# Second expert layer: value projections a quarter later, and pools that wait tile by tile for the stage before

## The chip, the cores and the metric

The program runs on one core of a Trainium2 chip. The core has five engines, each of which works off its own list of instructions in order: PE (TensorE, matrix products into PSUM), DVE (VectorE), ACT (ScalarE), POOL (GpSimd) and SP (SyncE, which here only issues DMA transfers). The metric is the device time of one execution in microseconds (us), the median of three runs. Everything is float32.

## The reference

The input `x` has 4 batches of 512 tokens with 256 channels. Four layers are added to it in turn: a cross attention, a mixture of experts, a second cross attention with a long convolution and a feed-forward net, and an attention whose value and output projections are chosen among eight experts. The change is in this last layer:

```python
# x: layer-normed input (4, 512, 256); H = 16 heads, DH = 64, E = 8 experts, K = 2
q = einsum('btc,hdc->bhtd', x, Wq);  k = einsum('btc,hdc->bhtd', x, Wk)
w, sel = top_k(einsum('btc,hec->bthe', x, Ws), K)            # two experts per token and head
mix_v  = einsum('bthk,bthke->bthe', sigmoid(w), one_hot(sel, E))
proj_v = einsum('btc,edc->bted', x, Wv)                      # a value per token and expert
v      = einsum('bthe,bted->bhtd', mix_v, proj_v)            # mixed for each head
probs  = softmax(einsum('bhid,bhjd->bhij', q * DH**-0.5, k))
attn   = einsum('bhij,bhjd->bihd', probs, v)
_, sel_o = top_k(einsum('btc,hec->bthe', x, Wd), K)
mask_o = one_hot(sel_o, E).sum(axis=3)
out    = einsum('bthe,bthd,efd->bthf', mask_o, attn, Wo).sum(axis=2)
```

## The kernel before

The four layers are four stages, one after the other. Each stage opens its own pools of SBUF and PSUM memory and closes them at its end, so a stage's pools lie where those of the stages before lay. The tokens `xr` (16 tiles of 128 tokens) stay in SBUF throughout.

**The stage before, "the old stage" below** (lines 1820 to 2009), is the second cross attention's convolution and feed-forward. Its SBUF pools are `y_w` (weights, in the order `fwd` 16 KB for each partition, `wfi` and `wfo` 4 KB each, a few bytes of `gate`, six rows of 1 KB among which `row_go` and `row_bo`, `inv` 16 KB, and more), `y_1` and `y_2`. Ahead of them lies the pool `keep`, with 4 KB of `kT4` and 16 KB of `ctT`, 20.5 KB in all. Its PSUM pools are `y_a` (six banks) and `y_t` (two). For each batch it ends with the products `po` (L2001), their addition (L2002), a layer norm into `yo` (ACT, L1908 and L1909), two operations of POOL that scale and shift `yo` with `row_go` and `row_bo` (L2005, L2006) and four POOL additions into `xr` (L2008).

**The last stage** (lines 2014 to 2252) opens `d_w` (weights), `d_1`, `d_2` (two buffers for each tag), `d_3` (four buffers of the tag `tmp`) in SBUF, and `d_m` (four single banks: `mm`, `pp`, `acc`, `ao`), `d_s` and `d_t` (two each) in PSUM. A pool is opened by default so that whoever first touches one of its tiles waits until all the work on every older pool under it is done. The four weights `d_wv`, `d_wq`, `d_wk` and `d_wo` (4, 8, 8 and 4 KB) are loaded on SP's queue at L2027. The order of PE, DVE and ACT is the order of the program text (`manual_schedule`); POOL and SP are ordered by the planner.

A *pair* `u` is two heads of one batch, eight pairs for each batch, 32 in all. A pair is worked off in four *quarters* `c`. In each quarter the loop at L2216 writes, in this order:

1. `scores(u + 1, c)`: two products `pss` on PE, for each a row maximum `dnm` on DVE (L2119) and an exponential `pe` on ACT (L2121). The bank ring of `pss` has two slots.
2. In quarters 1 and 2, `by_expert(u - 1)`: in quarter 1 a transpose `ao` on PE, two small DVE operations `drs` and `dmw`, and in each of the two quarters two DVE products `tmp2` (L2169, tag `tmp`) with a POOL addition each into `agg` (L2170).
3. A share of the *fill*, the preparation of the next batch (below).
4. In quarters 0 and 2, half of `pair_in(u + 2)`: the query or key product (`pq`, `pk`, L2070 and L2076) in the bank `mm` and its copy by ACT.
5. Output products of the batch before, now and then.
6. `transposed(u, c)` and `gather`: PE transposes with copies by ACT, and the product with the values.

The fill for the next batch is `batch_in(b + 1)`: layer norm, gates, choice of the experts, and then four times `mixed(b, qt)`, one for each 128 tokens. `mixed` makes the value projection `pp` (L2047, one bank, one buffer), and mixes it for all heads: a DVE product for each of eight experts e, the first (L2057) straight into the value tile `dv`, the other seven (L2060) into a `tmp` buffer, from which POOL adds it into `dv` (L2061). `tmp` and `tmp2` share one ring of four buffers, so DVE can be four such products ahead of POOL, no more.

Each step of the fill yields its cost in the author's own units. In each quarter `upto` (L2185) takes steps while its credit is above zero; a quarter's credit is 7.2, 1.3, 1.3 and 7.2 for c = 0 to 3, and what is overdrawn is carried on. Written out, this places the value projection of the first tile (`qt` = 0) of the next batch in quarter 0 of pair 3, and those of the other three in quarter 0 of pairs 4, 5 and 6, each directly behind the last product (e = 7) of the tile before it, which reads the same bank. The last three products of the fourth tile are in quarter 0 of pair 7.

For the very first batch there is no earlier stage to hide the fill in: `mixed(0, 0)` is interleaved with the first scores (L2203 to L2207) and the other three are run whole in the quarters of pair 0 (L2225).

Of the kernel before, what the change touches and what calls it, by code (L numbers as in the profile page):

```python
# [752 lines left out]
def kernel(ctx: ExitStack, tc: tile.TileContext, a: dict, out: bass.AP):  # L753
# [115 lines left out]
    with ExitStack() as st:  # L869
        p1 = st.enter_context(tc.tile_pool(name="f_1", bufs=1))  # L870
# [949 lines left out]
    with ExitStack() as st:  # L1820
        wp = st.enter_context(tc.tile_pool(name="y_w", bufs=1))
        p1 = st.enter_context(tc.tile_pool(name="y_1", bufs=1))
        p2 = st.enter_context(tc.tile_pool(name="y_2", bufs=2))
# [188 lines left out]


    with ExitStack() as st:
        wp = st.enter_context(tc.tile_pool(name="d_w", bufs=1))
        p1 = st.enter_context(tc.tile_pool(name="d_1", bufs=1))
        p2 = st.enter_context(tc.tile_pool(name="d_2", bufs=2))
        p3 = st.enter_context(tc.tile_pool(name="d_3", bufs=4))
        ps_m = st.enter_context(tc.tile_pool(name="d_m", bufs=1, space=PSUM))
        ps_s = st.enter_context(tc.tile_pool(name="d_s", bufs=2, space=PSUM))  # L2020
        ps_t = st.enter_context(tc.tile_pool(name="d_t", bufs=2, space=PSUM))
# [20 lines left out]

        def mixed(b, qt):

            pp = ps_m.tile([P, SE, SD], F32, name="pp", tag="pp")
            for k in range(2):
                nc.tensor.matmul(  # L2047
                    pp.rearrange("p e d -> p (e d)"), xnTs[b][:, k, qt * P : (qt + 1) * P], wv[:, k, :],
                    start=(k == 0), stop=(k == 1),
                )  # L2050
            yield 0.8
            v_t = p2.tile([P, SH, SD], F32, name=f"dv{qt}", tag=f"dv{qt}")
            for e in range(SE):
                m_w = mixes[b][:, qt * SH : (qt + 1) * SH, e].unsqueeze(2).to_broadcast([P, SH, SD])
                p_w = pp[:, e, :].unsqueeze(1).to_broadcast([P, SH, SD])
                if e == 0:
                    tt(v_t, p_w, m_w, ALU.mult)  # L2057
                else:
                    tmp = p3.tile([P, SH, SD], F32, name="tmp", tag="tmp")
                    tt(tmp, p_w, m_w, ALU.mult)  # L2060
                    nc.gpsimd.tensor_tensor(v_t, v_t, tmp, ALU.add)  # L2061
                yield 2.2
            vs[b, qt] = v_t
# [44 lines left out]
        def scores(u, it):  # L2108
            qT, kT = qks[u]
            if it == 0:  # L2110
                sums[u] = small.tile([P, QT, 2], F32, name="dsums", tag="dsums")
                nms[u] = small.tile([P, QT, 2], F32, name="dnm", tag="dnm")
            pss = [ps_s.tile([P, S], F32, name="pss", tag="pss") for _ in range(2)]
            for j in range(2):
                rows = slice(64 * j, 64 * j + SD)
                nc.tensor.matmul(pss[j], qT[rows, it * P : (it + 1) * P], kT[rows, :], start=True, stop=True)  # L2116
            for j in range(2):
                nm = nms[u][:, it, j : j + 1]
                nc.vector.tensor_reduce(nm, pss[j], AX.X, ALU.max, negate=True)  # L2119
                pe = p2.tile([P, S], F32, name="pe", tag=f"pe{it}{j}")  # L2120
                nc.scalar.activation(pe, pss[j], AF.Exp, bias=nm, accum_out=sums[u][:, it, j : j + 1])  # L2121
                pes[u, it, j] = pe
# [62 lines left out]
        def upto(g, us):  # L2185

            while us > 0:
                n = next(g, None)
                if n is None:
                    return 0.0  # L2190
                us -= n
            return us

        def batch_in(b):
            yield from inputs(b)
            yield from gates_in(b)
            yield from gates(b)
            for qt in range(QT):
                yield from mixed(b, qt)

        run(pair_in(0))
        scores(0, 0)
        fill = mixed(0, 0)  # L2203
        for c in range(1, QT):
            upto(fill, 4.0)
            scores(0, c)
        run(fill)  # L2207
        run(pair_in(1))
        values0 = [mixed(0, qt) for qt in range(1, QT)]
        outs = iter(())  # L2210
        ins = {}
        fill, credit = iter(()), 0.0
        experts = iter(())
        for u in range(NP + 1):
            b, m = divmod(u, NH)
            for c in range(QT):  # L2216
# [9 lines left out]
                if (m, c) == (1, 0) and b + 1 < B:  # L2226
                    fill, credit = batch_in(b + 1), 0.0
                if m:

                    credit = upto(fill, credit + (1.7, 0.3, 0.3, 1.7)[c] * FILL / STEPS)  # L2230
# [126 lines left out]
```

## Time and profile before

| | us |
|---|---|
| median of 3 runs (lowest, highest) | 3442.59 (3435.63, 3444.97) |
| profiled execution, its own time | 3443.15 |
| its span, first to last instruction | 3441.0 |
| PE busy (share of the span) | 2920.9 (85%) |
| DVE busy | 2301.1 (67%) |
| ACT busy | 1606.6 (47%) |
| POOL busy | 1001.1 (29%) |
| mean granted TensorE clock | 0.910 |

The old stage ends and the last stage begins at about 2540 us of the span, so the last stage is some 900 us of it. The shares above are means over four quite different stages. In the lines of the profile L is a line of the kernel, `out<-in` are tiles, and `[idle before <-releaser]` is how long the engine had stood idle and what ended that. A line of the timeline may merge several like instructions (x2, x7); its two first numbers are then the start of the first and the time to the end of the last.

### The profile page before, as it was taken

The page shows a single profiled execution, that of the slowest core. Times are in us where ns is not written, and L with a number is a line of the kernel's source. Part 1 is how long each engine was busy: PE and PEld are TensorE (multiplying, and loading weights), DVE is VectorE, ACT ScalarE, POOL GpSimd, SP SyncE. Part 2 cuts the span into 40 slices and gives each one's busy share as a digit, 9 for nine tenths or more (in the row PEclk, how much of TensorE's full clock was granted, in tenths as well). Part 3 has the DMA queues.
Part 4 walks back from the last instruction along what each step waited for, and adds up shares of the span by engine and source line. Part 5 has one row for each costly group of instructions (what it writes and reads, how often), then busy time and mean ns, then how long its engine had stood idle before and what let it go on. Part 6 is the DMA issues. An engine that isn't in the chain of part 4 may idle for free. (4 is left out here: it accounts for less than half of the span.)

```text
span 3441.0 us, 42208 instructions
## 1 busy us (share of the span) xinstructions
PE 2920.9 (85%) x15886; PEld 1637.5 (48%) x15886; DVE 2301.1 (67%) x3887; ACT 1606.6 (47%) x3307; POOL 1001.1 (29%) x747
## 2 busy tenths in 40 slices
PE   7999999999968996787978776789766888788798
PEld 3333333333347983565555555566533334344354
DVE  7666666666468984989989896343445765657654
ACT  2555555555625773555555553122323454454454
POOL 2011001100016763100000000133335781845835
PEclk9999999999958998988889998899887898898899
DMA  3001000000017882000000002100000000000000
GB/s 83 25 14 28 4 11 14 14 8 7 2 56 240 286 280 69 26 15 1 1 15 1 1 1 56 50 0 1 0 37 0 1 1 7 1 4 4 1 7 7
DMA packets 59156, 118.25 MB, mean 34 GB/s; under 512 B 16594, under 2 KB 32732, under 8 KB 58940
## 3 DMA queue, kind: packets, MB, share of 16 engines
q0 software_dynamic: 24736, 74.46, 6.9%
q1 hardware_dynamic: 33564, 40.43, 3.9%
q8 instruction: 129, 2.11, 0.3%
q14 instruction: 87, 0.71, 0.1%
q10 hardware_dynamic: 640, 0.54, 0.1%
HBM read 97.16 MB, written 9.31 MB: 31 GB/s over the span
## 5 line engine op out<-in xcount | busy, mean ns | idle before, releaser
L265 DVE TENSOR_REDUCE mx<-pss 128x1 f32<-128x512 f32 x768 | 492.6, 684 | 261.7 <-PE pss L261 257.8
L311 ACT ACTIVATE pT<-pst 128x512 f32<-128x512 f32 (+1 forms) x832 | 449.8, 596 | 405.3 <-PE pss L261 299.4
L308 PE MATMUL pst<-qm,kT 32*128 32x512 f32 (+1 forms) x1664 | 507.3, 635 | 1.4 <-ACT pT L311 0.7
L261 PE MATMUL pss<-kT,qT 32*128 32x512 f32 x1536 | 494.0, 642 | 4.1 <-DMA kT<-kc 3.5
L1113 PE MATMUL sum<-dg,e 128*128 128x128 f32 (+1 forms) x1664 | 265.3, 322 | 129.2 <-ACT dg L1089 128.9
L2170 POOL TENSOR_TENSOR agg<-agg,tmp 128x1024 f32<-128x1024 f32 x112 | 263.2, 2381 | 278.8 <-DVE tmp L2169 278.7
L1113 PEld LDWEIGHTS sum<-dg,e 128*128 128x128 f32 (+1 forms) x1664 | 237.3, 225 | 186.3 <-ACT dg L1089 154.3
L2121 ACT ACTIVATE pe<-pss,dnm 128x512 f32<-128x512 f32 x256 | 173.5, 683 | 270.5 <-DVE dnm L2119 270.3
L2119 DVE TENSOR_REDUCE dnm<-pss 128x1 f32<-128x512 f32 x256 | 164.5, 683 | 176.8 <-PE pss L2116 176.4
L2061 POOL TENSOR_TENSOR dv<-dv,tmp 128x1024 f32<-128x1024 f32 x112 | 262.9, 2349 | 62.0 <-DVE tmp L2060 38.5
L308 PEld LDWEIGHTS pst<-qm,kT 32*128 32x128 f32 (+1 forms) x1664 | 150.7, 180 | 267.5 <-ACT pT L311 242.8
L318 PE MATMUL acc<-pT,v 128*32 128x512 f32 (+1 forms) x1664 | 221.7, 605 | 0.3 <-ACT ou L325 0.3
L2116 PE MATMUL pss<-dkT,dqT 64*128 64x512 f32 x512 | 169.0, 659 | 25.2 <-ACT pe L2121 23.8
L169 POOL DMA_DIRECT2D qT<-qc x28 | 13.7, 496 | 578.4 <-DVE qc L232 578.1
L261 PEld LDWEIGHTS pss<-kT,qT 32*128 32x128 f32 x1536 | 149.2, 185 | 33.5 <-issue 22.9
L800 POOL TENSOR_TENSOR ln_rs<-ln_ve,nhalf 128x4 f32<-128x4 f32 x32 | 34.0, 1062 | 435.2 <-DVE ln_neg L1905 371.8
L2130 ACT COPY dpT<-tp 128x512 f32<-128x512 f32 x256 | 138.1, 595 | 46.5 <-PE tp L2128 46.5
L1591 PE MATMUL pa<-xgT,wb 128*128 128x128 f32 x1248 | 155.4, 279 | 2.4 <-ACT xgT L1584 2.4
L1559 POOL DMA_INDIRECT wb<-in_f_w,w_at x117 | 137.9, 1179 | 65.4 <-issue 19.8
L2060 DVE TENSOR_TENSOR tmp<-pp,mix 128x1024 f32<-128x1024 f32 x112 | 134.1, 1218 | 30.7 <-POOL dv L2061 23.1
L1022 PE MATMUL pss<-xkT,xqT 64*128 64x512 f32 (+1 forms) x512 | 148.4, 600 | 4.9 <-ACT sc L1029 3.1
L1591 PEld LDWEIGHTS pa<-xgT,wb 128*128 128x128 f32 x1248 | 149.4, 195 | 6.0 <-ACT xgT L1584 3.1
(419 smaller groups left out, 5591.4 us busy)
## 6 DMA issues: line engine op xcount, KB each, us to landing
c<-in_ctxT SPq DMA_DIRECT2D x8, 800.5 KB
ys<-yo SPq DMA_DIRECT2D x39, 128.0 KB
c<-in_ctxT SPq DMA_DIRECT2D x8, 400.2 KB
kT<-kc SPq DMA_DIRECT2D x96, 32.0 KB
kT<-kc POOLq DMA_DIRECT2D x84, 32.0 KB, 2.2
xr<-in_x SPq DMA_DIRECT2D x16, 128.0 KB
xs<-xn SPq DMA_DIRECT2D x4, 512.0 KB
fwd<-in_dft SPq DMA_DIRECT2D x1, 2048.0 KB
```

The lines of the kernel that those rows point to most:

```text
L261: nc.tensor.matmul(pss[:, :wd], qT[rows[j], qt * P : (qt + 1) * P], kT[rows[j], o : o + wd], start=True, stop=True,)
L265: nc.vector.tensor_reduce(mx[:, gi, qt, j, n : n + 1], pss[:, :wd], AX.X, ALU.max)
L308: nc.tensor.matmul(pst[:wd, :], kTs[gi % 4][rows, c * P : c * P + wd], qms[gi][rows, :], start=True, stop=True)
L311: nc.scalar.activation(pT[:wd, j, :], pst[:wd, :], AF.Exp)
L318: nc.tensor.matmul(acc[32 * j : 32 * j + 32, :], vs[b][:wd, c, AG * g + j, :], pT[:wd, j, :], start=(c == 0), stop=(c == NG - 1), tile_pos ...
L1113: nc.tensor.matmul(pm[:w, c - 4 * n, :], e[:, c * P : c * P + w], dg, start=(h == 0 and c == 4 * n), stop=(h == 3 and c == cols[-1]),)
L1591: nc.tensor.matmul(pa[:, c, :], wbs[i, half][:, o : o + P], xTs[i][:, k, :], start=(k == 0), stop=(k == 1))
L2061: nc.gpsimd.tensor_tensor(v_t, v_t, tmp, ALU.add)
L2116: nc.tensor.matmul(pss[j], qT[rows, it * P : (it + 1) * P], kT[rows, :], start=True, stop=True)
L2119: nc.vector.tensor_reduce(nm, pss[j], AX.X, ALU.max, negate=True)
L2121: nc.scalar.activation(pe, pss[j], AF.Exp, bias=nm, accum_out=sums[u][:, it, j : j + 1])
L2170: nc.gpsimd.tensor_tensor(aggs[b][it], aggs[b][it], tmp2, ALU.add)
```

## The change

1. The four SBUF pools of the last stage are opened with `reuse_waits="tile"`: a tile that is first touched waits for the work on those old tiles that lay under it, and no longer for all work on the old pools. The three PSUM pools stay as they were.
2. `mixed` yields a step of cost 0.0 before its projection `pp`.
3. `upto` stops a quarter's share of the fill when it meets that 0.0; the credit that is left goes to the next quarter. The places where fills are run whole (`run`) pass over it.
4. The first fill of the stage, `mixed(0, 0)`, is advanced past its 0.0 once, so it starts as before.

With the credits written out again, the four projections of batches 1, 2 and 3 move from quarter 0 to quarter 1 of pairs 3, 4, 5 and 6. With each go the products that followed it in that quarter (three, two, one and one), to quarter 1 too, behind that quarter's scores, `ao` and its first two `tmp2`. From quarter 2 on every step stands where it stood, and the fill ends in quarter 0 of pair 7 in both.

```diff
-        wp = st.enter_context(tc.tile_pool(name="d_w", bufs=1))
-        p1 = st.enter_context(tc.tile_pool(name="d_1", bufs=1))
-        p2 = st.enter_context(tc.tile_pool(name="d_2", bufs=2))
-        p3 = st.enter_context(tc.tile_pool(name="d_3", bufs=4))
+        wp = st.enter_context(tc.tile_pool(name="d_w", bufs=1, reuse_waits="tile"))
+        p1 = st.enter_context(tc.tile_pool(name="d_1", bufs=1, reuse_waits="tile"))
+        p2 = st.enter_context(tc.tile_pool(name="d_2", bufs=2, reuse_waits="tile"))
+        p3 = st.enter_context(tc.tile_pool(name="d_3", bufs=4, reuse_waits="tile"))
...
         def mixed(b, qt):
 
+            yield 0.0
             pp = ps_m.tile([P, SE, SD], F32, name="pp", tag="pp")
...
                 n = next(g, None)
                 if n is None:
                     return 0.0
+                if n == 0.0:
+                    break
                 us -= n
             return us
...
         fill = mixed(0, 0)
+        next(fill)
         for c in range(1, QT):
             upto(fill, 4.0)
             scores(0, c)
```

## The prediction

> **What bounds the kernel now.** I read the page first, then the boundary between the two stages in the timeline, then who waits for whom inside the last stage, and last POOL's own timeline, since those waits pointed to it.
>
> The page's busy times come first (engine, busy us, share, instructions).
>
> ```profile
> PE 2920.9 (85%) x15886; PEld 1637.5 (48%) x15886; DVE 2301.1 (67%) x3887; ACT 1606.6 (47%) x3307; POOL 1001.1 (29%) x747
> ```
>
> PE's 85% is a mean over stages and says little about either place that the change touches. The first is the boundary; these are lines of the timeline around 2540 us.
>
> ```profile
> 2525.21 0.42 DVE L2002 TENSOR_TENSOR xt<-po,xt 128x256 f32<-128x256 f32 x1 [3.03 <-PE po L2001]
> ...
> 2531.92 0.51 ACT L1909 ACTIVATE yo<-yo,ln_rs 128x256 f32<-128x256 f32 x1
> ...
> 2534.98 2.34 POOL L2006 TENSOR_TENSOR yo<-yo,row_bo 128x1024 f32<-128x1024 f32 x1
> 2537.34 0.38 SPq L2027 DMA_DIRECT2D d_wv<-in_d_wv  x1
> 2537.39 2.77 POOL L2008 TENSOR_TENSOR xr<-xr,yo 128x256 f32<-128x256 f32 x4
> 2537.77 0.46 SPq L2027 DMA_DIRECT2D d_wq<-in_d_wq  x1
> ...
> 2544.10 3.39 PE L2070 MATMUL pq<-dxT,d_wq 128*128 128x512 f32 x4 [18.99 <-DMA d_wq<-in_d_wq]
> 2547.65 0.60 ACT L2072 ACTIVATE dqT<-pq 128x512 f32<-128x512 f32 x1 [15.22 <-PE pq L2070]
> 2548.30 1.98 PE L2076 MATMUL pk<-dxT,d_wk 128*128 128x512 f32 x4 [0.81 <-ACT dqT L2072]
> ...
> 2552.13 1.29 DVE L2119 TENSOR_REDUCE dnm<-pss 128x1 f32<-128x512 f32 x2 [24.09 <-PE pss L2116]
> ```
>
> PE stands still for 18.99 us until a weight arrives, and that transfer is issued as soon as POOL is through with L2006, the last reader of the old pools under `d_w`. DVE waits 24.09, ACT 15.22: nothing else runs here, so the boundary is on the path of the whole program.
>
> The second place is the fill. In the waits of the last stage's three fills, the projection stands out (us in total, times, longest):
>
> ```profile
> PE pp L2047 <- DVE tmp L2060: 59.2, 9, 8.7
> ```
>
> PE stands nine times before `pp`, because DVE still reads its bank. What that costs is seen on POOL, in the fill of the last batch:
>
> ```profile
> 3145.78 4.78 POOL L2061 TENSOR_TENSOR dv<-dv,tmp 128x1024 f32<-128x1024 f32 x2 [11.95 <-DVE tmp L2060]
> 3150.53 9.28 POOL L2170 TENSOR_TENSOR agg<-agg,tmp 128x1024 f32<-128x1024 f32 x4
> 3159.78 14.36 POOL L2061 TENSOR_TENSOR dv<-dv,tmp 128x1024 f32<-128x1024 f32 x6
> 3175.66 9.29 POOL L2170 TENSOR_TENSOR agg<-agg,tmp 128x1024 f32<-128x1024 f32 x4 [1.52 <-DVE tmp L2169]
> ...
> 3202.99 4.67 POOL L2170 TENSOR_TENSOR agg<-agg,tmp 128x1024 f32<-128x1024 f32 x2 [3.61 <-DVE tmp L2169]
> ...
> 3233.16 9.31 POOL L2170 TENSOR_TENSOR agg<-agg,tmp 128x1024 f32<-128x1024 f32 x4 [4.16 <-DVE tmp L2169]
> ...
> 3259.32 9.30 POOL L2170 TENSOR_TENSOR agg<-agg,tmp 128x1024 f32<-128x1024 f32 x4
> ```
>
> From 3145.78 to 3268.62 POOL rests only three times, 9.29 us in 122.84. It takes some 2.35 us for an addition, DVE 1.2 for the product behind it, and DVE stalls on the ring of four. In the fills POOL is the bound, and the PE waits matter only by POOL's gaps.
>
> **The change, part by part.** The sum is made against the profiled execution, 3443.15 us (span 3441.0, 2.15 around it), 0.56 above the median.
>
> *Weights, tile by tile.* By the sizes in the code, `d_w` (24 KB) lies on `keep` (20.5 KB) and the first 3.5 KB of `fwd`. The last reads of those are PE's: `kT4` by L1875 (last matmul at 2156.4), `ctT` by L1897 (2407.0), `fwd` by L1949 (2457.1). So the four issues (0.38 to 0.47 us each on SP) come between 2157 and 2458 and land by 2465 at the 5.9 us that `d_wq` took. SP's own rows have nothing between the last old load (2156.3) and 2537, so nothing queues behind their waits; the engines' DMA share in 2200 to 2400 is 0.00. Cost nothing; the cover is 60 us of old-stage products.
>
> *The first chain.* What is late next? PSUM still waits for its whole old pool: DVE's read at 2525.21 + 0.42 = 2525.63. There `pq` starts, warm, as PE stopped at 2525.1: 1.98 like the `pk` row, to 2527.6. Its copy `dqT` stands on ACT behind the last L1909, which ends at 2531.92 + 0.51 = 2532.43; with 0.60 it ends at 2533.03, and `pk`, which needs the same bank, starts at 2533.1. PE has then been idle 5.4 us. The row nearest to that is `pq` after 18.99 us (3.39 against 1.98), so I take 3.39: end 2536.5; `dkT` (0.58) 2537.1; `pss` (1.13) 2538.3; `dnm` starts at 2538.4 instead of 2552.13. Gain 13.7; with a warm `pk` 15.1, the upper bound. If the first chain were held until POOL's last old instruction ends (2537.39 + 2.77 = 2540.16), `dqT` would come at 2540.2 and not 2547.65: 7.4. If no wait goes, 0.
>
> The Trainium skill, "TensorE: Matmul & The Clock Gate" (section "Part 1: The HAM clock gate"), lets the clock fall to half after an idle window of about 3.4 us; by it `pk` is cold and the sum is the same 13.7, and the trace agrees, with a `pss` group that takes 2.74 and not 1.13 after 2.57 idle.
>
> *The other tiles of the first pairs.* `dqT` and `dkT` lie on `fwd` and `wfi`, free by 2458. The first `dv` lies on `row_go` and `row_bo`, so DVE's L2057 waits for L2006 (2537.32); it is due at 2554.24 − 13.7 = 2540.5. POOL's first `dv` addition is due at 2556.81 − 13.7 = 2543.1, and POOL is free at 2540.16. Slack 2.9: nothing. More semaphore waits may be written: the rows have 51 ns for one; 40 first touches on three engines would be 2 us if all were on the path, they are not, so 0.
>
> *Pair 0.* `run` passes the 0.0 and `mixed(0, 0)` is advanced by hand, so the two PE waits there (75.6 us in the whole stage less 59.2) stay.
>
> *The fills.* Twelve projections move by a quarter: on PE from ahead of `pq` to behind the next scores and `ao`; on DVE three, two, one and one products move behind two `dnm`, `drs`, `dmw` and two `tmp2`; their POOL additions (two, one, none, none; e = 0 has none) move behind two `agg` additions. No DMA moves. Nine projections had waited; what queued behind them was `pq`, transposes, the next scores, and with these DVE's next `tmp2` and so POOL.
>
> Now take quarter 0 of pair 4 in the last fill. The product e = 7 ends on DVE at 3162.18 + 1.21 = 3163.4, with POOL busy until 3174.1. Before, `pp` (3.78, cold), `pq` 2.27, transposes 0.87, `gather` 1.01, `pss` 1.11, two `dnm`, `drs`, `dmw` and a `tmp2` came in line: POOL's next work was ready at 3175.6. After, the scores of quarter 1 are already there, and DVE needs `dnm` 1.28, `drs` 0.19, `dmw` 0.23 to 2.33, `tmp2` 1.24: 3 to 5 us, where POOL has 9 to 11 in stock. The gap goes; likewise the two others. So POOL's gaps inside the fills are the gain: 1.52 + 1.83 + 3.86 + 4.29 = 11.5 in batch 1, 1.52 + 3.65 + 4.17 = 9.3 in batch 2, and 9.3 in batch 3: 30.1.
>
> Against it stands a later start. POOL's first instruction was the `dv` addition at 3145.78; now the first `tmp2` must come first. `ao` ended at 3146.3, set by ACT's copies and not by `pp`; with DVE's 1.24 POOL starts at 3147.6: 1.8 late, the same in batch 2. In batch 1 `pp` stood cold on PE's path; there I work out 2697.0 for 2692.84: 4.1. Sum 7.7, so the fills gain 30.1 − 7.7 = 22.4. Upper bound 30.1 (no late start); lower bound −7.7 (late start, no gap closed). I take 22.4, as the stock of 9 us exceeds the 5 by far. PE's wait is gone too, but is not counted again.
>
> The sum: 3443.15 − 13.7 − 22.4 = 3407.
>
> **The rivals.**
>
> A. *Only POOL's tail is waited for at the boundary* (7.4): 3443.15 − 7.4 − 22.4 = 3413. For it: `dv` does lie on tiles that POOL reads late. Against: that reader ends 3 us before it is needed.
>
> B. *The pools keep waiting as a whole*, so the first part doesn't do what it says: 3443.15 − 22.4 = 3421. For it: nothing in the trace of before shows a tile-wise wait across these stages.
>
> C. *DVE is held by POOL's reads once POOL has no gaps.* `dmw` takes 0.23 beside an idle POOL and 2.33 at 3252.26 beside a busy one. At the nine places, 2.1 us each on the path make 18.9, and the fills gain 3.5: 3426. Against: the ring's stock covers 2.1 us. The Trainium skill, "SBUF — State Buffer" (section "Who interferes with whom"), says that a DVE instruction with two SBUF inputs contends with a POOL instruction that reads SBUF, for the whole instruction; the two `dmw` rows agree.
>
> D. *Slower: POOL runs dry before the later value products.* Place: quarter 1 of pairs 4 to 6. A quarter there lasts 112/16 = 7 us (four pairs in 3145 to 3257). If POOL rests one quarter at each of nine places, in place of the mean 30.1/9 = 3.3, that is 3.7 × 9 = 33 lost and 7.7 for the starts: 3443.15 − 13.7 + 33 + 7.7 = 3470. It decides once the way from e = 7 to the next `tmp2` exceeds POOL's stock of 9 us; I find 3 to 5.
>
> E. *No effect* (B, and the gaps come back elsewhere): 3443.
>
> **How the numbers follow.** Forecast 0.64, A 0.07, B 0.08, C 0.09, D 0.07, E 0.05. The forecast's own range is 3398 (15.1 and 30.1 gained) to 3417 (13.7 and 12). Nine tenths of it are 0.58; with A, B and C, up to 3430, that is 0.82, and D and E stay out: 3398 to 3430. About 0.3%, 10 us, is what a measurement can tell from no change: faster is forecast, A, B and C, 0.88; same 0.05; slower 0.07.
>
> **What would show it.** Right: weights issued before 2460; `pq` at about 2525.7 and the first `dnm` of the last stage near 2538.4; PE's wait of `pp` for `tmp` in the fills near 0 instead of 59.2; POOL without gaps over 0.5 us from the first `agg` of each fill for some 113 us; its first fill instruction an `agg`. Wrong: weights still issued at 2537 (B), `dqT` at 2540 (A), `dmw` over 2 us right ahead of a POOL gap (C), or gaps of POOL ended by `tmp` in quarter 1 (D).

## The result, and the profile after

The changed kernel takes 3401.09 us (median of 4 runs, 3398.85 to 3402.53); the kernel before took 3443.78 us beside it (4 runs). The ratio is 0.9882, with a 95% interval of 0.9867 to 0.9897: some 43 us less, where the forecast of 3407 had 36. The profiled execution took 3400.68 us (span 3398.9), against 3443.15 (3441.0).

Both executions can be cut at the same events, so that the parts add up to the span. The cut between the stages is the start of the old stage's last DVE instruction (L2002); a "fill" runs from POOL's first `agg` addition behind a long rest (57 to 64 us between two fills) to the end of the `agg` additions behind the fill's last `dv`.

| stretch, us | before | after | difference |
|---|---|---|---|
| three old stages, to L2002 | 2525.21 | 2525.77 | +0.6 |
| from there to the first fill | 145.65 | 132.00 | −13.65 |
| fill of batch 1, 2, 3 | 147.09, 145.32, 145.28 | 138.87, 137.91, 138.40 | −8.22, −7.41, −6.88 |
| the stretch behind each fill | 80.06, 80.01, 49.98 | 81.64, 75.60, 49.80 | +1.58, −4.41, −0.18 |
| last batch, to the end of its last `agg` | 99.83 | 99.87 | 0.0 |
| from there to the end | 22.57 | 19.04 | −3.5 |
| span | 3441.0 | 3398.9 | −42.1 |

The busy times after (engine, busy us, share, instructions; those of before stand in the prediction):

```profile
PE 2930.2 (86%) x15886; PEld 1639.0 (48%) x15886; DVE 2316.5 (68%) x3887; ACT 1606.9 (47%) x3307; POOL 1001.4 (29%) x747
```

The counted instructions are the same; no engine became cheaper. DVE is even busy for 15.4 us more, of which more below. What went is waiting. First the weights, in SP's queue of the changed kernel (start, us, line, out and in):

```profile
2158.45 0.38 SPq L2027 DMA_DIRECT2D d_wv<-in_d_wv  x1
2238.34 0.38 SPq L2027 DMA_DIRECT2D d_wq<-in_d_wq  x1
2408.29 0.37 SPq L2027 DMA_DIRECT2D d_wk<-in_d_wk  x1
2458.10 0.37 SPq L2027 DMA_DIRECT2D d_wo<-in_d_wo  x1
```

All four are issued 67 us or more ahead of 2525, as soon as the old tiles under each are read; before, the first came at 2537.34. Then the boundary in the timeline of the changed kernel (start, us, engine, line, tiles; in brackets the idle time before and what ended it):

```profile
2525.77 0.42 DVE L2002 TENSOR_TENSOR xt<-po,xt 128x256 f32<-128x256 f32 x1 [3.03 <-PE po L2001]
2526.25 1.98 PE L2071 MATMUL pq<-dxT,d_wq 128*128 128x512 f32 x4 [0.59 <-DVE xt L2002]
...
2532.49 0.51 ACT L1909 ACTIVATE yo<-yo,ln_rs 128x256 f32<-128x256 f32 x1
...
2532.90 0.58 ACT L2073 ACTIVATE dqT<-pq 128x512 f32<-128x512 f32 x1
...
2533.53 3.78 PE L2077 MATMUL pk<-dxT,d_wk 128*128 128x512 f32 x4 [5.30 <-ACT dqT L2073]
...
2537.97 2.77 POOL L2008 TENSOR_TENSOR xr<-xr,yo 128x256 f32<-128x256 f32 x4
...
2539.05 1.98 PE L2048 MATMUL pp<-d_wv,dxT 128*128 128x512 f32 x4
2539.15 1.29 DVE L2120 TENSOR_REDUCE dnm<-pss 128x1 f32<-128x512 f32 x2 [10.55 <-PE pss L2117]
...
2541.13 1.23 DVE L2058 TENSOR_TENSOR dv<-pp,mix 128x1024 f32<-128x1024 f32 x1 [0.69 <-POOL xr L2008]
...
2543.56 16.90 POOL L2062 TENSOR_TENSOR dv<-dv,tmp 128x1024 f32<-128x1024 f32 x7 [2.82 <-DVE tmp L2061]
```

`pq` no longer waits for a DMA but for the one old DVE instruction, since the PSUM pools still wait as a whole. Its copy `dqT` stands behind the last old L1909 on ACT, and `pk` behind that copy, after 5.30 us of idle PE, at nearly half speed (3.78 against 1.98 us for `pq`). The first `dnm` is 13.38 us behind L2002; before it was 26.92 behind. The row of the first `dv` names POOL's L2008 for its 0.69 us of waiting, but `dv` starts 0.39 us behind the end of L2008 (2540.74) and only 0.10 behind that of its own product `pp` (2541.03), and in e9_dve_first below it starts before L2008 does. So it is `pp` that it waits for here.

From the start of the first fill to the end of the last, the waits of PE (us in total, times, longest) have no row of `pp` any more, and this one in its place:

```profile
PE pss L2117 <- ACT pe L2122: 36.5, 31, 4.2
```

Before, over the same stretch, that row had 12.1 us. PE waits elsewhere, and that costs nothing as long as POOL always has an addition to do. POOL's own timeline of the changed kernel, in the last fill:

```profile
3116.61 4.67 POOL L2171 TENSOR_TENSOR agg<-agg,tmp 128x1024 f32<-128x1024 f32 x2 [14.33 <-DVE tmp L2170]
3121.25 4.79 POOL L2062 TENSOR_TENSOR dv<-dv,tmp 128x1024 f32<-128x1024 f32 x2
3125.99 4.68 POOL L2171 TENSOR_TENSOR agg<-agg,tmp 128x1024 f32<-128x1024 f32 x2
3130.60 12.12 POOL L2062 TENSOR_TENSOR dv<-dv,tmp 128x1024 f32<-128x1024 f32 x5
3142.67 4.68 POOL L2171 TENSOR_TENSOR agg<-agg,tmp 128x1024 f32<-128x1024 f32 x2
...
3203.98 16.94 POOL L2062 TENSOR_TENSOR dv<-dv,tmp 128x1024 f32<-128x1024 f32 x7
3220.87 9.32 POOL L2171 TENSOR_TENSOR agg<-agg,tmp 128x1024 f32<-128x1024 f32 x4
```

From 3116.61 to 3220.87 + 9.32 = 3230.19, that is for 113.58 us, POOL has no gap at all; before it had three, 9.29 us together. The first instruction is now an `agg`, and the idle time ahead of it is 14.33 instead of 11.95: the later start.

Why POOL does not run dry is seen on DVE at one of the moved places, quarter 0 to 1 of pair 4, in the changed kernel:

```profile
3133.03 1.22 DVE L2061 TENSOR_TENSOR tmp<-pp,mix 128x1024 f32<-128x1024 f32 x1
3134.55 1.36 DVE L2120 TENSOR_REDUCE dnm<-pss 128x1 f32<-128x512 f32 x2 [0.29 <-PE pss L2117]
3135.82 0.19 DVE L2155 RECIPROCAL drs<-dsums 128x8 f32<-128x8 f32 x1
3136.05 1.88 DVE L2157 TENSOR_TENSOR dmw<-mo,drs 128x64 f32<-128x64 f32 x1
3138.06 2.36 DVE L2170 TENSOR_TENSOR tmp<-ao,dmw 128x1024 f32<-128x1024 f32 x2
3140.33 1.22 DVE L2058 TENSOR_TENSOR dv<-pp,mix 128x1024 f32<-128x1024 f32 x1
```

The last product of the old tile (e = 7) ends at 3133.03 + 1.22 = 3134.25 and the first `tmp2` half way through the group of 3138.06, at about 3139.2. POOL works on its `dv` additions until 3142.67. So the way takes 5.0 us where POOL had 8.4 in stock.

### The profile page after: what moved, and what is told of

It reads as the page before. It is cut to its first block, busy times and chain, and to the rows that moved or that the text cites. A ratio compares the mean times of both kernels' runs of the same rounds, so it can differ in the third digit from the quotient of the medians.

```text
span 3398.9 us, 42222 instructions
## 1 busy us (share of the span) xinstructions
PE 2930.2 (86%) x15886; PEld 1639.0 (48%) x15886; DVE 2316.5 (68%) x3887; ACT 1606.9 (47%) x3307; POOL 1001.4 (29%) x747
## 5 line engine op out<-in xcount | busy, mean ns | idle before, releaser
L2117 PE MATMUL pss<-dkT,dqT 64*128 64x512 f32 x512 | 181.7, 671 | 47.7 <-ACT pe L2122 46.3
L2129 PEld LDWEIGHTS tp<-ident,pe 128*128 128x128 f32 x1024 | 127.1, 150 | 61.5 <-issue 38.8
```

## The experiments

The times of whole runs scatter by 10 us and more, and much of that lies in the stages that no kernel here touches: the start of the last L2002 lies anywhere from 2518.10 to 2530.33 us in the eleven profiled executions. So sizes are read from the cut of the table above. Each kernel has one profiled execution, but where two kernels have the same code in the boundary or in a fill, their lengths agree to 0.1 us. The medians only say whether they agree.

**One half alone.** Before with the four pools' `reuse_waits`, and the changed kernel without them:

```diff
 e1_pools (on before)
-        wp = st.enter_context(tc.tile_pool(name="d_w", bufs=1))
+        wp = st.enter_context(tc.tile_pool(name="d_w", bufs=1, reuse_waits="tile"))
...
 e2_order (on the changed kernel)
-        wp = st.enter_context(tc.tile_pool(name="d_w", bufs=1, reuse_waits="tile"))
+        wp = st.enter_context(tc.tile_pool(name="d_w", bufs=1))
...
```

> Only the four pools wait tile by tile; the fill's order is that of before. If the two parts are independent: the first row maximum of the last stage comes 13 us earlier than before, POOL's gaps in the fills stay as they were (11.5, 9.3 and 9.3 us), and the time falls by 13 to 14 us against before. If instead the boundary gain only counts because the fills behind it changed as well, less than 5 us.

> Only the order of the fill; the pools wait as a whole. Theory, POOL's gaps are the gain: PE still stands still for 19 us until d_wq has landed, the gaps inside the fills go, and the time falls by about 22 us (8.2, 7.4 and 6.9 in the three fills of the changed kernel). Together with the pools alone that is 36 us; the changed kernel gained 6 more, and if those come from the granted clock in stretches that nothing touched, the two parts need not add up to better than 6 us. Rival, the two parts help each other: they add up to less than 30.

Measured: e1_pools 3424.54 us against 3444.43 (0.9945, 0.9928 to 0.9961), e2_order 3410.22 (0.9892, 0.9863 to 0.9922). By the cut, e1_pools takes 131.99 us from L2002 to the first fill, as the changed kernel does, and its fills are those of before: 147.10, 145.31, 145.30. From L2002 to the end it gains 915.79 − 902.08 = 13.7, as expected; the medians have 19.9, with an interval of 13 to 25. The wait for the bank is all there, as the row of PE's waits in its fills says:

```profile
PE pp L2047 <- DVE tmp L2060: 59.2, 9, 8.8
```

e2_order is the reverse: 145.64 us from L2002, and fills of 138.81, 137.86 and 138.34. Its boundary shows the old wait:

```profile
2521.97 0.43 DVE L2002 TENSOR_TENSOR xt<-po,xt 128x256 f32<-128x256 f32 x1 [3.03 <-PE po L2001]
...
2540.90 3.36 PE L2071 MATMUL pq<-dxT,d_wq 128*128 128x512 f32 x4 [19.04 <-DMA d_wq<-in_d_wq]
```

From L2002 to the end e2_order gains 29.2: 22.7 in the fills, as expected, and 6.5 in the stretches behind them and the tail, where the changed kernel has the same 6.5 (below). So the two parts do not touch each other: 13.7 and 29.2 make 42.9, and the changed kernel gains 42.7 there. The medians alone could not show it, as they add to 54.

**What the ring's depth is worth, with and without the move.** One size, once on before and once on the changed kernel:

```diff
-        p3 = st.enter_context(tc.tile_pool(name="d_3", bufs=4))
+        p3 = st.enter_context(tc.tile_pool(name="d_3", bufs=3))
```

> The kernel before, with three tmp buffers and not four, so POOL's stock is 7 us and not 9.4. Theory, before lost time where POOL ran dry while PE's projection waited: each gap grows by one addition, 2.35 us, at the ten gaps of the three fills, and new ones open: 24 to 30 us slower than before. Rival, PE's own waits of 59 us are the cost and POOL is only busy beside them: under 8 us.

> The changed kernel with three tmp buffers. Theory: from the last product of a value tile to the next tmp product DVE now needs 3 to 5 us, which a stock of 7 us still covers, so POOL stays nearly without gaps: 0 to 8 us slower than the changed kernel, a third or less of what the same edit costs the kernel before. Rival, the ring couples DVE and POOL in the same way in both orders: the same 24 to 30 us in both.

Measured: 3461.64 us (1.0053, 1.0033 to 1.0074), some 17 us slower, where 24 to 30 were expected; and 3409.48 (0.9907, 0.9876 to 0.9938), 8 over the changed kernel. By the cut, the fills of before grow by 5.4, 5.7 and 7.7 us, 18.8 in all. POOL's gaps in the last one, in e3_ring3_before:

```profile
3185.01 9.30 POOL L2170 TENSOR_TENSOR agg<-agg,tmp 128x1024 f32<-128x1024 f32 x4 [4.00 <-DVE tmp L2169]
...
3215.58 4.67 POOL L2170 TENSOR_TENSOR agg<-agg,tmp 128x1024 f32<-128x1024 f32 x2 [6.87 <-DVE tmp L2169]
...
3247.39 9.30 POOL L2170 TENSOR_TENSOR agg<-agg,tmp 128x1024 f32<-128x1024 f32 x4 [5.80 <-DVE tmp L2169]
```

They were 1.52, 3.61 and 4.16. Each grew by 1.6 to 3.3, about the one addition of 2.35 us by which POOL's stock is smaller. So a gap was the way from e = 7 to the next `tmp2`, less the stock. In e4_ring3_after the same step costs the fills nothing (137.73, 137.82, 137.87, none with a gap after its start): 5.0 us of way are less than the stock of three as well. What it loses lies in the stretches behind the fills (83.94, 84.04 and 52.15 for 81.64, 75.60 and 49.80): 13.1 us more, of which some 3 are made up elsewhere. In the second stretch some 6 us of it are PE's clock (0.79 for 0.88, below); the other 2.3 in each were not traced. The expectation for the first kernel had the sign and the mechanism, and was too large.

**Is POOL the bound in the fills now?** One addition of seven is left out for each tile:

```diff
-                    nc.gpsimd.tensor_tensor(v_t, v_t, tmp, ALU.add)
+                    if b == 0 or e < SE - 1:
+                        nc.gpsimd.tensor_tensor(v_t, v_t, tmp, ALU.add)
```

> The changed kernel without POOL's addition of expert 7 in the fills of batches 1 to 3: the product is still made on DVE, but its share is missing from the values of these batches. It takes 12 additions of 2.35 us, 28.2 us, from POOL and nothing from any other engine. Theory, POOL bounds the fills: 20 to 28 us faster than the changed kernel. Rival, PE or DVE bounds them since the change: under 6 us.

Measured: 3379.27 us (0.9811, 0.9793 to 0.983), 22 below the changed kernel. The fills shrink by 9.7, 9.8 and 10.2 us, for four additions of 2.35 = 9.4 that each no longer does: what POOL is spared is gained in full, and it still has no gap inside the fills. DVE, PE and ACT have the same instructions as in the changed kernel. Of those 29.7 us, 6.5 are given back in the stretches behind (84.42, 76.61, 52.46).

**Does DVE's longer `dmw` cost anything (rival C)?** In the fills' `dmw` rows (count, ns lowest/median/highest, first and last start), the first of before and the second of the changed kernel:

```profile
L2156 DVE TENSOR_TENSOR dmw<-mo,drs x21: 224/225/2333, 2696.2 to 3252.3; 128x64 f32<-128x64 f32 x21
```

```profile
L2157 DVE TENSOR_TENSOR dmw<-mo,drs x21: 224/1878/2356, 2681.4 to 3213.8; 128x64 f32<-128x64 f32 x21
```

The median went from 0.225 to 1.878 us: rival C saw the effect rightly. The Trainium skill, "SBUF — State Buffer" (section "Who interferes with whom"), has DVE instructions with two SBUF inputs contend with POOL's reads, and these rows agree. The next kernel takes `drs` and `dmw` away in most pairs of the fills:

```diff
-            rs = small.tile([P, QT, 2], F32, name="drs", tag="drs")
-            nc.vector.reciprocal(rs, sums[u])
-            mw = small.tile([P, QT, 2, SE], F32, name="dmw", tag="dmw")
+            mw = mos[b].rearrange("p (q h) e -> p q h e", q=QT)[:, :, 2 * m : 2 * m + 2, :]
+            if m < 2 or m == 7 or b == B - 1:
+                rs = small.tile([P, QT, 2], F32, name="drs", tag="drs")
...
```

> The changed kernel without drs and dmw in the 15 pairs whose outputs are mixed during a fill, so these outputs are not divided by their softmax sums. In the changed kernel dmw takes a median of 1.88 us there and not 0.23. Theory, the ring's stock covers it and POOL is the bound: 0 to 4 us faster than the changed kernel. Rival C of the prediction, DVE held behind POOL lies on the path: 15 times some 2 us, 20 to 30 us faster.

Measured: 3403.1 us (0.9879, 0.9854 to 0.9903), against 3401.09 for the changed kernel. The fills shrink by 0.57, 0.03 and 0.46 us. Rival C falls: the effect is there and is covered by POOL's stock. Outside the fills this kernel is slower than the changed one, by 10.5 us in the stretches behind them (82.10, 83.94 and 51.54) and by 1.8 in the tail; in the second stretch PE's granted clock is 0.76 for 0.88, of which more below.

**What is late next at the boundary.** The two copies of pair 0 are moved from ACT, whose queue still holds old work, to DVE:

```diff
-            nc.scalar.mul(qT, pq, SD**-0.5)
+            if u == 0:
+                nc.vector.tensor_scalar(qT, pq, SD**-0.5, None, ALU.mult)
+            else:
+                nc.scalar.mul(qT, pq, SD**-0.5)
...
-            nc.scalar.copy(kT, pk)
+            (nc.vector.tensor_copy if u == 0 else nc.scalar.copy)(kT, pk)
```

> The changed kernel with dqT and dkT of pair 0 made by DVE instead of ACT, whose queue still holds the last tile's four additions L1909 when pq is there. Theory (ACT's queue is what is late next at the boundary, and behind it POOL's old tail): the first dnm comes about 6 us earlier after the last old DVE instruction (13.4 to about 7.5 us), but the first dv of the layer still needs the slot that POOL's last old instruction L2008 frees at 15 us after it, so POOL's first addition moves by about 3 us and the whole gains 2 to 4 us. Rival (pair 0 alone sets the pace behind the boundary, POOL does not hold it): the whole 6 us are kept. Second rival (the copies cost DVE, which is the bound there): no gain, the first dnm at 13 us or later.

Measured: 3396.66 us against 3447.54 (0.986, 0.9843 to 0.9877). The boundary in its timeline:

```profile
2523.71 0.42 DVE L2002 TENSOR_TENSOR xt<-po,xt 128x256 f32<-128x256 f32 x1 [3.03 <-PE po L2001]
...
2527.19 1.98 PE L2080 MATMUL pk<-dxT,d_wk 128*128 128x512 f32 x4 [1.01 <-DVE dqT L2074]
...
2531.11 1.29 DVE L2123 TENSOR_REDUCE dnm<-pss 128x1 f32<-128x512 f32 x2 [1.22 <-PE pss L2120]
...
2535.86 1.23 DVE L2058 TENSOR_TENSOR dv<-pp,mix 128x1024 f32<-128x1024 f32 x1 [3.45 <-POOL yo L2006]
2535.90 2.77 POOL L2008 TENSOR_TENSOR xr<-xr,yo 128x256 f32<-128x256 f32 x4
...
2538.63 16.89 POOL L2062 TENSOR_TENSOR dv<-dv,tmp 128x1024 f32<-128x1024 f32 x7
```

`pk` comes after 1.01 us of idle PE instead of 5.30 and runs in 1.98; `dnm` is 7.40 us behind L2002 instead of 13.38. Of these 5.98 us the whole keeps 873.13 − 869.59 = 3.5, and POOL's first addition moves by 2.87: it now starts where POOL's last old instruction ends (2535.90 + 2.77 = 2538.67). DVE's first `dv` now waits 3.45 us for POOL's L2006, the last reader of the old tiles under it, and not for L2008, as the expectation had it. ACT's queue was what was late next, and POOL's old tail stands right behind it.

**A version that beats both.** In the changed kernel POOL still rests 14.33 us ahead of the last fill. Here the fill begins one pair earlier (in the first batch with pair 1), and its credit is spread over the longer stretch:

```diff
-        STEPS = NH * QT - 6
+        STEPS = NH * QT - 2
...
-                if (m, c) == (1, 0) and b + 1 < B:
+                if c == 0 and (u == 1 or u > 1 and m == 0) and b + 1 < B:
...
-                if m:
+                if u > 0:
```

> A version meant to beat both: the changed kernel with each fill begun in pair 0 of a batch (pair 1 in the first) and not in pair 1, with quarter credits scaled to 30 steps and not 26, so that POOL's additions are spread over more pairs. Theory, POOL is the bound only while the fills run, 113 us for each of three, and stands idle for some 60 us before each: the additions move into that idle time and the time falls by 15 to 30 us against the changed kernel. Rival, the pairs that receive the earlier steps are bound by PE and DVE and lose as much: within 5 us.

Measured: 3373.78 us (0.9804, 0.9773 to 0.9835), 69 below before; by the cut, 20.5 below the changed kernel. POOL at the start of the last fill, in e8_early:

```profile
3087.68 14.55 POOL L2062 TENSOR_TENSOR dv<-dv,tmp 128x1024 f32<-128x1024 f32 x6 [4.58 <-DVE tmp L2061]
...
3111.43 2.34 POOL L2062 TENSOR_TENSOR dv<-dv,tmp 128x1024 f32<-128x1024 f32 x1
3115.20 9.68 POOL L2062 TENSOR_TENSOR dv<-dv,tmp 128x1024 f32<-128x1024 f32 x4 [1.43 <-DVE tmp L2061]
```

The rest of 14.33 us has become 4.58, as POOL has additions of the fill to do in it, and one gap of 1.43 is new. Nearly all of the gain is in the fills of batches 2 and 3 (128.60 and 128.73 us for 137.91 and 138.40); the first, which begins where it began, takes 139.00. Last, the same with the two copies on DVE:

> The kernel whose fill begins a pair earlier (label e8_early) with the same two copies of pair 0 on DVE. Theory: in it the first addition of the expert layer on POOL is what follows the boundary directly, so the gain of the copies is again bounded by POOL's last old instruction: 2 to 4 us less than e8_early, 3368 to 3374 us. Rival (the whole 6 us are kept): about 3366 us. Rival (no gain): 3373 us or more.

Measured: 3381.05 us (0.981, 0.979 to 0.9831), over the 3368 to 3374 of the theory and, by the median, where the rival of no gain has it. By the cut, however, it is 2.6 us better than e8_early (849.98 against 852.60 from L2002 to the end), and all of that is at the boundary (131.70 for 134.36 to the first fill), as the theory had it. The medians, taken on different chips beside a before of 3447.54 and of 3442.73, cannot show so little: against their own before the two ratios, 0.9804 and 0.981, are the same. So one profiled execution of each, and no more, shows that the copies add to e8_early.

## Why the prediction was right, point by point

*Boundary*: the time from L2002 to the first fill shrank by 13.65 us, for 13.7 in the sum. The steps hold one by one: `pq` behind DVE's last old read (2526.25; L2002 came 0.56 later in this execution), `dqT` behind the last L1909, `pk` cold. Only the price of `pk` was taken too low, 3.39 for 3.78. That the sum fits to 0.1 us all the same is in part luck, as small errors cancel: the first `dnm` gained 13.54 and POOL's first addition 13.81. The Trainium skill, "TensorE: Matmul & The Clock Gate" (section "Part 1: The HAM clock gate"), has PE's clock fall to half after an idle window; `pk` agrees, with 3.78 us after 5.30 idle and, in e9_dve_first, 1.98 after 1.01. The `pss` group that the prediction cites for it agrees in the half speed alone: its products took 1.06 to 1.22 us for 0.59 to 0.69, but after 2.57 us of idle time, which is shorter than the window that the prediction names. There the measurement decides.

*The slack of 2.9 us* between POOL's old tail and its first addition is the 2.87 that e9_dve_first could gain on POOL before the tail held it. Here rival A was near: with pair 0 three microseconds earlier it would have been the limit. In the changed kernel nothing waits for it.

*Fills*: 22.51 us for 22.4. The gaps that went are 30.1, and the later starts took 3.32, 1.92 and 2.38 (14.87 − 11.55, 13.87 − 11.95, 14.33 − 11.95) for 4.1, 1.8 and 1.8.

*Rivals.* B and E fall with the issues at 2158 to 2458; C falls with e6_no_dmw. D was far off: at the place shown the way is 5.0 us, at the upper end of the 3 to 5 that were worked out, POOL's stock there 8.4 instead of 9 to 11, and with one buffer fewer POOL still does not run dry.

*What was not in the sum* is the rest of the 42.1 us of span: 3.0 in the stretches behind the fills and 3.5 in the tail (and 0.6 lost ahead). These run the same instructions in both kernels. The forecast had taken them as unchanged, and that is its largest error, 6.5 us in the kernel's favour. e2_order has these 6.5 us and e1_pools has none of them, so they came with the moved projections, but by PE's clock (next section) and not by a wait that the change takes away: they are luck.

## What the runs showed of the hardware

Stretches that are not changed take different times because of PE's clock. The first place is the stretch between two fills. These are two windows of before and two of the changed kernel (stretch, length, busy us and instructions of PE, PEld, DVE, ACT, POOL, then the granted clock, the share of DMA and GB/s), each POOL's long rest between two fills:

```profile
2835.00:2898.00 63.00, 47.30 (x200) 29.43 (x200) 23.32 (x38) 26.65 (x60) 1.02 (x1) 0.81 0.02 7
3060.00:3124.00 64.00, 47.92 (x204) 29.72 (x204) 24.32 (x40) 27.31 (x61) 1.67 (x2) 0.81 0.02 7
```

```profile
2813.50:2878.50 65.00, 49.27 (x202) 31.40 (x204) 23.55 (x39) 26.99 (x60) 1.24 (x2) 0.79 0.02 7
3033.00:3092.00 59.00, 43.21 (x202) 26.41 (x204) 23.61 (x39) 26.79 (x60) 1.23 (x2) 0.88 0.02 7
```

In the changed kernel the same 202 products take 49.27 us at a granted clock of 0.79 in one window, and 43.21 at 0.88 in the next, and the second window is 6 us shorter. POOL's idle time there is 63.48 and 57.42 us in the changed kernel, 63.54 and 57.44 in e2_order, 63.48 and 57.42 in e9_dve_first, but 61.72 and 61.67 in before, 61.70 and 61.66 in e1_pools. It goes with what was written ahead of it and repeats to 0.1 us between kernels with the same fills, so it is no noise. A small edit of the fills is enough to change it: the second rest is 63.50 us in e4_ring3_after, 64.05 in e6_no_dmw and 55.77 in e5_no_add7.

The second place is the tail, of before and then of the changed kernel:

```profile
3411.57 3.78 PE L2087 MATMUL tpa<-ident,agg 128*128 128x128 f32 x16 [4.87 <-POOL agg L2170]
3416.03 3.78 PE L2096 MATMUL po<-d_wo,aT 128*128 128x256 f32 x8 [0.68 <-ACT aT L2092]
3420.42 3.76 PE L2087 MATMUL tpa<-ident,agg 128*128 128x128 f32 x16 [0.61 <-DVE ot L2100]
```

```profile
3372.97 3.78 PE L2088 MATMUL tpa<-ident,agg 128*128 128x128 f32 x16 [4.88 <-POOL agg L2171]
3377.43 1.99 PE L2097 MATMUL po<-d_wo,aT 128*128 128x256 f32 x8 [0.68 <-ACT aT L2093]
3380.03 2.02 PE L2088 MATMUL tpa<-ident,agg 128*128 128x128 f32 x16 [0.61 <-DVE ot L2101]
```

Both begin with a slow group after the same wait (4.87 and 4.88 us), and the clock comes back behind one group in the changed kernel and behind three in before: 1.8 us for each of two groups, the 3.5 of the table. e1_pools ends like before (22.50 us), e2_order and e9_dve_first like the changed kernel (18.98 and 19.02). But the order on PE does not settle it: e3_ring3_before, with that of before, has one slow group and 18.60 us, and e6_no_dmw, with that of the changed kernel, has two and 20.83. What decides was not tried; it stays open.

The other number is that DVE's busy time grew by 15.4 us at no cost to the fills. The 32 `dmw` alone went from 17.0 to 33.3 us: one that waits beside POOL for 1.65 us more (the two medians above) counts as busy in the profile, and by e6_no_dmw nobody waits for it.

## What to carry to other kernels

Where one engine sets the pace through a ring of buffers, count a stall upstream of it only by the gap that it leaves on that engine: the way from the last buffer written to the next, less the stock that the ring holds; moving independent work of the same ring into the stall closes the gap, and then a longer way costs nothing until the stock is spent. At a boundary between stages, ask of each wait that goes which queue is late next: here the weights hid an ACT queue worth 3.5 us, and that hid POOL's old tail. And a few microseconds in stretches that no edit touched can be PE's clock; cut the executions at common events before crediting them to the change.
